# Graph network layer on one core: attention scores in single PSUM banks, and single-row source fetches by SyncE for eleven blocks instead of six

## Chip, core and metric

One core of one Trainium2 chip. The metric is the time of one execution in device microseconds: 1613.16 us in the median of three runs before the change (1609.63 to 1617.16).

## What is computed

```python
ea  = edge_attr @ w_e + b_e                       # 131072 edges, 64 -> 256 features
msg = relu(x[src] + ea)                           # x: 8192 nodes x 256
agg = segment_sum(msg, dst, 8192)                 # dst is sorted
t   = x + agg
h_local = bn1(relu(t @ w1 + b1) @ w2 + b2 + x)
# attention in 256 groups of 32 nodes, 4 heads of 64
q, k, v = split(x @ in_w.T + in_b)
attn = softmax(q @ k.T / 8);  h_attn = bn2((attn @ v) @ out_w.T + out_b + x)
out = h_local + h_attn
out = bn3(out + relu(out @ m_w1 + m_b1) @ m_w2 + m_b2)
return layernorm(x + out)
```

## The kernel before

All is float32. The edges come in 128 **blocks** of 1024 (`BE`), in order of `dst`; a block's sums fall on about 64 nodes. The nodes come in 16 **chunks** of 512, so a chunk goes with 8 blocks. The stages of a block `b`:

- POOL fetches the source rows with 8 gathers of 128 rows (`gather`, line 217) into the tile `xs`, from `x` at first, and from block 20 on from `xb`, a copy of `x` with the edge bias added. Each gather is held back by a semaphore until TensorE has reached a mark in its own list, by planned times (`hold_fetches`).
- SyncE loads the edge features `ea` with four DMAs (`load_edges`, line 264; four buffers).
- VectorE transposes `ea` in 32x32 squares into `eaT` (`edge_transpose`, line 281; two buffers).
- TensorE multiplies `eaT` with the weights (`edge_products`) into two PSUM tiles `pe` of two banks each; the tag `pe` has two buffers, four banks. All matmuls are recorded at line 174.
- VectorE adds `xs` and `pe` (`edge_messages`, line 338, two adds of 1024 columns; called **adds** below), ScalarE applies relu (line 342).
- VectorE builds a one-hot `oh` of the destinations (`edge_hot`, line 350; two buffers), and TensorE sums the messages with it into `pw` (**sums**). ScalarE copies `pw` to `ws` (line 385), and TensorE places `ws` into `l2` with a second one-hot. VectorE adds that to the chunk's `xT` (line 409).

Beside this run, chunk by chunk, the attention (`attention_front`, `attention_back`) and the dense layers with the layer norm (`dense`; its last step is a reciprocal of `rstd`, line 730, and four scalings of `y`, line 732, and SyncE's store of `y`). Their PSUM tiles, `pw` and `l2` have the tag `at`: four buffers of one bank. In `attention_back` the scores of two heads are multiplied into one tile of two banks (`bank2()`, so with the tag `pe`), and ScalarE copies the blocks on its diagonal to `pr` with four copies of 256 columns for two heads (line 617).

**Single rows.** For the blocks in `FETCHED`, the last of the eight gathers is left out, and SyncE fetches these 128 rows with one DMA each from `xb` into a tile `xf` of its own (`row_stream`, line 242; two buffers), 16 rows in a step. A step begins with the load of 16 addresses into registers (line 235). `fetch_rows` allows `RUN` steps per block from block `FROM` on, and `some_rows` issues them. The add of such a block's last quarter is made in three pieces (line 332).

**What sets the order.** TensorE's list is in the order of the code. Up to block 104 (`TAIL`) the code goes by pairs of blocks: sums of block b-2, products of b, sums of b-1, then adds of b, a share of attention and dense work (`Work.run`), one-hot and products of b+1, and so on. From block 104 on, a small planner in the code picks the next piece of work, block by block, by planned times (`came`, `added`, `summed_at`). VectorE's and ScalarE's lists are in the order of the code up to block 24 (`NV`). From there on, and for SyncE throughout, the build's scheduler decides where an instruction stands, by its own planned times and by what an instruction depends on; on the chip each engine then takes its list strictly in order.

Of the kernel before, what the change touches and what calls it, by code (L numbers as in the profile page):

```python
# [19 lines left out]
P = 128  # L20
# [21 lines left out]
RUN = 0.75  # L42
RL = 4
FETCHED = [44, 54, 64, 76, 86, 98]
FROM = 26
# [39 lines left out]
def gnn_kernel(ctx: ExitStack, tc: tile.TileContext, x, src, dst, edge_attr, w, out):  # L85
# [121 lines left out]

    def gather(b):
        xs = epool.tile([P, NH, TJ, C], FP, name="xs", tag="xs", bufs=BUFS)
        for h in range(NH):  # L210
            for j in range(TJ):
                if b in FETCHED and h * TJ + j == TB - 1:
                    continue
                idx = srcd[:, b * NH + h, j : j + 1] if b < ND else srci[:, b, h * TJ + j : h * TJ + j + 1]
                fetches.append((
                    b * TB + h * TJ + j,
                    nc.gpsimd.indirect_dma_start(  # L217
                        out=xs[:, h, j, :],
                        out_offset=None,
                        in_=x if b < NX else xb[:, :],  # L220
                        in_offset=bass.IndirectOffsetOnAxis(ap=idx, axis=0),
                    ).ins,
                ))
# [4 lines left out]
    xf_of = {}  # L228

    def row_stream():  # L230

        for b in FETCHED:
            xf = xf_of[b] = epool.tile([P, C], FP, name="xf", tag="xf", bufs=2)
            for r in range(0, QR, RL):
# [5 lines left out]
                for i, at in enumerate(rows):  # L240
                    p = i % EQ * QR + r + i // EQ
                    nc.sync.dma_start(xf[p : p + 1, :].bitcast(U8), xb_bytes[:, ds(at, C * 4)])  # L242
                yield
# [71 lines left out]
    def edge_messages(b, pairs=range(0, NH, 2), of_pair=range(2)):  # L315
# [6 lines left out]
        for h in pairs:  # L322
            pe = pe_of[b, h]
            for u in of_pair[::n]:
                hs = slice(h + u, h + u + n)
                if h + u + n == NH and b in FETCHED:
                    for us, js, rows in (
# [255 lines left out]
    def attention_back(st, pool, bank, bank2):  # L583
# [18 lines left out]
        for hh in range(H // 2):  # L602
            two = bank2()
            for t in range(TN):
                for s in range(2):
                    a = t * P
                    matmul(
                        two[:, s, a : a + P],
# [5 lines left out]
            two4 = two.rearrange("p s (t k) -> p s t k", t=TN)  # L614
            for g in range(GT):
                q = slice(g * NPG, (g + 1) * NPG)
                nc.scalar.copy(pr[q, :, 2 * hh : 2 * hh + 2, :].rearrange("p t s k -> p s t k"), two4[q, :, :, q])
# [224 lines left out]
    class Work:  # L842
# [69 lines left out]
    with tc.manual_schedule(engines={PE}):  # L912
# [9 lines left out]
        for c in range(NCH):  # L922
# [10 lines left out]
            work.add(BACK, lambda s=st: s.get("front"), attention_back(st, npool, bank, bank2))  # L933
# [116 lines left out]
        came = [8.7 + 10.035 * (i + 1) for i in range(NB)]  # L1050
# [88 lines left out]
    with tc.If(wide > 0):  # L1139
# [67 lines left out]
        with tc.tile_pool(name="gfin", bufs=1) as pool, tc.tile_pool(name="gfin_ps", bufs=1, space=PSUM) as ps_pool:  # L1207
# [4 lines left out]
            def gbank2():  # L1212
                return ps_pool.tile([P, 2, CH], FP, name="gat2", tag="gat2", bufs=2)

            with tc.For_i(0, N, CH) as n0:
# [3 lines left out]
                for _ in attention_back(st, pool, gbank, gbank2):  # L1219
                    pass  # L1220
# [38 lines left out]
```

## Time and profile before

| | |
|---|---|
| median of three runs | 1613.16 us |
| profiled execution, its own time | 1610.6 us |
| its span, first to last instruction | 1608.8 us |
| mean granted TensorE clock | 0.911 |
| bytes read from and written to HBM | 222.13 MB and 16.78 MB |
| share of 16 DMA engines taken by POOL's gathers | 30.9% |
| and by SyncE's queue | 22.6% |

PE is TensorE, PEld its weight loads, DVE VectorE, ACT ScalarE, POOL GpSimd, SP SyncE. A line of a group reads: line, engine, operation, tile written <- tiles read, shapes, count | busy us, mean ns of one | idle us of the engine just before them, with what ended most of it. A line of the timeline reads: start us, length us, engine, line, operation, tiles, shapes, count, and in brackets the idle time before it with what ended it. "Issue" and "remote" are waits whose end the profile can't put down to an instruction. A matmul counts as two records, and its end is modelled. SP and the queues (SPq) have no busy time; their lines show from the first to the last issue. Fetches and transposes are told apart by block by counting them in the lists.

### The profile page before, as it was taken

The numbers are of one execution on the slowest core, as the hardware profiler recorded it, in microseconds if no ns is written. First come the engines' busy times: TensorE is split into PE (matmuls) and PEld (weight loads), VectorE is DVE, ScalarE is ACT, GpSimd is POOL, SyncE is SP. The second block draws the span as 40 slices with busy tenths as digits, with TensorE's granted clock in tenths as the row PEclk, the third lists the DMA queues.
The fourth block names the chain that finished last, engine by engine and source line by source line (L and its number), as shares of the span: only waits on it lengthen the run. The fifth ranks groups of instructions, "written<-read, shape, count | busy, mean of one in ns | idle before, by whom it ended". The sixth has DMA issues, their size and how long they took to land.

```text
span 1608.8 us, 23797 instructions
## 1 busy us (share of the span) xinstructions
PE 1325.8 (82%) x7671; PEld 769.9 (48%) x7671; DVE 804.0 (50%) x1643; ACT 588.3 (37%) x840; POOL 969.5 (60%) x1026
## 2 busy tenths in 40 slices
PE   4887898888988988987778777887788888888887
PEld 2444455444545444544445444454354444445465
DVE  4366554545445453463634536346363463645363
ACT  1333333343425333352433424325243253443233
POOL 6666565665666666666556565655665655666661
PEclk9798899899998999899899898899899999999999
DMA  9698765364645445355463564635548564545431
GB/s 230 181 298 267 215 181 135 112 168 116 170 130 163 126 129 156 99 144 146 122 159 103 150 150 123 160 100 154 144 116 196 141 161 123 158 136 145 118 105 51
DMA packets 150333, 240.57 MB, mean 150 GB/s; under 512 B 28638, under 2 KB 113788, under 8 KB 149436
## 3 DMA queue, kind: packets, MB, share of 16 engines
q0 software_dynamic: 48864, 133.50, 30.9%
q1 hardware_dynamic: 92860, 98.17, 22.6%
q10 hardware_dynamic: 8480, 7.35, 1.6%
q8 instruction: 62, 1.02, 0.3%
q14 instruction: 67, 0.55, 0.1%
HBM read 222.13 MB, written 16.78 MB: 148 GB/s over the span
## 4 chain that ended last, share of the span: by engine, by line
PE 35%; DVE 5%; issue 5%; another core or an unknown queue 3%; DMA 3%; ACT 1%; SPq 1%; POOL 0%; DVEq 0%; ACTq 0%; POOLq 0%
PE at L174 16%; PE pe L174 10%; PE pw L174 4%; PE l L174 3%; DMA xs<-xb,srci 2%; DVE xs L338 1%; PE at L763 1%; PE at L714 1%; DMA ea<-in_edge_attr_dram 1%; DVE eaT L281 1%; SPq L242 1%; DVE y L720 0%; PE at L178 0%; ACT xs L342 0%
## 5 line engine op out<-in xcount | busy, mean ns | idle before, releaser
L217 POOL DMA_INDIRECT xs<-xb,srci x858 | 814.7, 950 | 520.5 <-issue 200.6
L342 ACT ACTIVATE xs<-xs 128x1024 f32<-128x1024 f32 (+2 forms) x253 | 264.2, 1046 | 558.7 <-DVE xs L338 368.7
L338 DVE TENSOR_TENSOR xs<-pe,xs 128x1024 f32<-128x1024 f32 (+2 forms) x253 | 299.4, 1204 | 242.7 <-PE pe L174 72.3
L174 PE MATMUL pe<-we,eaT 64*128 64x256 f32 x2048 | 313.4, 440 | 120.4 <-issue 38.8
L174 PEld LDWEIGHTS pe<-we,eaT 64*128 64x128 f32 x2048 | 221.9, 214 | 231.4 <-issue 152.7
L174 PE MATMUL pw<-xs,oh 128*32 128x256 f32 x2048 | 183.6, 420 | 50.6 <-issue 35.8
L217 POOL DMA_INDIRECT xs<-in_x_dram,srci x144 | 137.5, 955 | 82.1 <-issue 44.0
L350 DVE TENSOR_TENSOR oh<-iota_n,rel 128x128 f32<-128x128 f32 x256 | 64.7, 291 | 212.7 <-PE pw L174 97.3
L174 PEld LDWEIGHTS pw<-xs,oh 128*32 128x32 f32 x2048 | 68.7, 116 | 165.3 <-issue 112.4
L174 PE MATMUL at<-xT,inT 128*128 128x512 f32 x256 | 124.5, 613 | 4.9 <-ACT qk L579 2.8
L174 PE MATMUL at<-hA,mw 128*128 128x512 f32 (+1 forms) x256 | 120.8, 598 | 1.1 <-issue 0.9
L174 PE MATMUL at<-m,mw 128*128 128x512 f32 (+1 forms) x256 | 118.3, 608 | 3.6 <-issue 2.5
L174 PE MATMUL l<-oh,ws 128*128 128x160 f32 (+4 forms) x512 | 88.1, 311 | 23.7 <-issue 11.9
L281 DVE STREAM_TRANSPOSE eaT<-ea 128x512 f32<-128x512 f32 x128 | 89.9, 702 | 32.5 <-PE pe L174 15.1
L409 DVE TENSOR_TENSOR xT<-l,xT 128x352 f32<-128x352 f32 (+14 forms) x107 | 43.4, 428 | 120.3 <-remote 35.7
L174 PEld LDWEIGHTS l<-oh,ws 128*128 128x128 f32 x512 | 75.0, 197 | 47.5 <-issue 28.0
L385 ACT COPY ws<-pw 128x512 f32<-128x512 f32 (+1 forms) x77 | 39.3, 510 | 118.5 <-remote 37.0
L174 PEld LDWEIGHTS at<-xT,inT 128*128 128x128 f32 x256 | 48.1, 195 | 66.4 <-issue 56.0
L174 PEld LDWEIGHTS at<-m,mw 128*128 128x128 f32 x256 | 50.6, 205 | 56.4 <-issue 50.7
L695 ACT ACTIVATE m<-at,vec 128x512 f32<-128x512 f32 (+1 forms) x64 | 41.9, 657 | 87.8 <-PE at L174 30.8
L174 PEld LDWEIGHTS at<-hA,mw 128*128 128x128 f32 x256 | 48.1, 200 | 52.8 <-issue 49.4
L174 PE MATMUL at<-oT,outT 128*128 128x512 f32 x128 | 64.3, 623 | 7.0 <-ACT oT L652 6.1
(157 smaller groups left out, 1295.7 us busy)
## 6 DMA issues: line engine op xcount, KB each, us to landing
ea<-in_edge_attr_dram SPq DMA_DIRECT2D x512, 128.0 KB
xs<-xb,srci POOLq DMA_INDIRECT x858
xf<-xb SPq DMA_DIRECT2D x768, 1.0 KB
xn<-in_x_dram ACTq DMA_DIRECT2D x14, 512.0 KB
out_dram<-y SPq DMA_DIRECT2D x14, 512.0 KB
xp<-in_x_dram SPq DMA_DIRECT2D x10, 512.0 KB
xb<-xp SPq DMA_DIRECT2D x10, 512.0 KB
xp<-in_x_dram SPq DMA_DIRECT2D x3, 1024.0 KB
```

The costliest lines, as they stand in the source:

```text
L174: mark(ps, nc.tensor.matmul(ps, *args, **kw).ins)
L217: nc.gpsimd.indirect_dma_start(out=xs[:, h, j, :], out_offset=None, in_=x if b < NX else xb[:, :], in_offset=bass.IndirectOffsetOnAxis(ap= ...
L242: nc.sync.dma_start(xf[p : p + 1, :].bitcast(U8), xb_bytes[:, ds(at, C * 4)])
L281: nc.vector.transpose(eaT, ea[:, QR:].rearrange("p (g d) -> p g d", d=ED)[:, :, :QR])
L338: nc.vector.tensor_add(msg[:, hs, js].rearrange("p u i c -> p i u c"), pe[:, js, u : u + n, :], xs[:, hs, js].rearrange("p u i c -> p i u c"),
L342: nc.scalar.activation(msg[:, hs, js], msg[:, hs, js], AF.Relu)
L350: nc.vector.tensor_tensor(oh[:, ts], iota_n[:, None, :WN].to_broadcast([P, TB // 2, WN]), rel[:, b, ts, None].to_broadcast([P, TB // 2, WN ...
L385: newest["ws"] = nc.scalar.copy(ws[:, :n], pw[:, :n]).ins
L409: newest["xT"] = nc.vector.tensor_add(xT, l2[:, :, a - n : z - n], xT).ins
L695: newest["relu"] = nc.scalar.activation(m1[:, o, :], layer(mw1, KC, o, hA), AF.Relu, bias=v_("m_b1", o)).ins
L714: nc.tensor.transpose(ps[:wt, t - t2, k * P : (k + 1) * P], zT[:, k, t * P : t * P + wt], ident)
L763: nc.tensor.matmul(ps[i], wt[:, k, o * P : (o + 1) * P], act[:, k, :], start=(k == 0), stop=(k == nk - 1))
```

## The change

1. The scores of two heads go to two tiles of one bank with the tag `at` instead of one tile of two banks with the tag `pe`. ScalarE copies each tile by itself: eight copies of 128 columns for two heads instead of four of 256, so 256 in all instead of 128. `bank2` is no longer handed to `attention_back`.
2. `FETCHED` has eleven blocks, 36, 44, ... 116, instead of 44, 54, 64, 76, 86 and 98, so POOL's gathers are 1013 instead of 1018. The steps begin at block 22 instead of 26, and each block has one instead of three in four blocks: 88 steps and 1408 rows instead of 48 and 768.
3. For the two of these blocks that lie in the tail (108 and 116), later gathers are dated one gather (1.254 us) earlier each, in `gather` and in the tail's `came`, and the planner lets rows be issued after each piece of work (`between()`).

```diff
-RUN = 0.75
+RUN = 1
...
-FETCHED = [44, 54, 64, 76, 86, 98]
-FROM = 26
+FETCHED = list(range(36, 120, 8))
+FROM = 22
...
+    def skipped(b):
+
+        return sum(TAIL <= i <= b for i in FETCHED)
...
-                    b * TB + h * TJ + j,
+                    b * TB + h * TJ + j - skipped(b - 1),
...
-            two = bank2()
+            two = [bank(), bank()]
...
-                        two[:, s, a : a + P],
+                        two[s][:, a : a + P],
...
-            two4 = two.rearrange("p s (t k) -> p s t k", t=TN)
-            for g in range(GT):
-                q = slice(g * NPG, (g + 1) * NPG)
-                nc.scalar.copy(pr[q, :, 2 * hh : 2 * hh + 2, :].rearrange("p t s k -> p s t k"), two4[q, :, :, q])
+            for s, ps in enumerate(two):
+                for g in range(GT):
+                    q = slice(g * NPG, (g + 1) * NPG)
+                    nc.scalar.copy(pr[q, :, 2 * hh + s, :], ps.rearrange("p (t k) -> p t k", t=TN)[q, :, q])
...
                         self.at[i], self.turn = t + 0.5, (i + 1) % n
+                        between()
                         return t
...
-        came = [8.7 + 10.035 * (i + 1) for i in range(NB)]
+        came = [8.7 + 10.035 * (i + 1) - 1.254 * skipped(i) for i in range(NB)]
```

What the build makes of it: TensorE's list is the same up to block 108, but for the names of the score tiles. VectorE's list changes from block 40 on. In the rows below a buffer's number tells the block; lines are those of each version.

VectorE at blocks 48 and 49, before (`oh_4883` is the one-hot of block 48, `eaT_4818` the transpose of block 50, `oh_4971` and `eaT_4904` those of 49 and 51):

```order
L350 TENSOR_TENSOR oh_4883<-iota_n_74,rel_87 128x128 x2
L338 TENSOR_TENSOR xs_4566<-pe_4791,xs_4566 128x2x2x256
L338 TENSOR_TENSOR xs_4566<-pe_4796,xs_4566 128x2x2x256
L281 STREAM_TRANSPOSE eaT_4818<-ea_4340 128x512
L350 TENSOR_TENSOR oh_4971<-iota_n_74,rel_87 128x128 x2
L660 SCALAR_TENSOR_TENSOR hA_3764<-at_4825,s2_101,hA_3764 128x512
L338 TENSOR_TENSOR xs_4575<-pe_4890,xs_4575 128x2x2x256
L338 TENSOR_TENSOR xs_4575<-pe_4895,xs_4575 128x2x2x256
L281 STREAM_TRANSPOSE eaT_4904<-ea_4446 128x512
```

The same place after the change (`eaT_5133` is the transpose of block 48 itself, `eaT_5252` that of 49):

```order
L357 TENSOR_TENSOR oh_5445<-iota_n_74,rel_87 128x128 x2
L287 STREAM_TRANSPOSE eaT_5133<-ea_4615 128x512
L345 TENSOR_TENSOR xs_5079<-pe_5354,xs_5079 128x2x2x256
L345 TENSOR_TENSOR xs_5079<-pe_5359,xs_5079 128x2x2x256
L357 TENSOR_TENSOR oh_5533<-iota_n_74,rel_87 128x128 x2
L667 SCALAR_TENSOR_TENSOR hA_4218<-at_5388,s2_101,hA_4218 128x512
L287 STREAM_TRANSPOSE eaT_5252<-ea_4703 128x512
L345 TENSOR_TENSOR xs_5088<-pe_5452,xs_5088 128x2x2x256
L345 TENSOR_TENSOR xs_5088<-pe_5457,xs_5088 128x2x2x256
```

A block's transpose has moved from behind the adds of two blocks before to directly ahead of its own adds, behind its own one-hot.

VectorE at block 70, where a chunk's layer norm and softmax lie (`eaT_6964`, and after it `eaT_7793`, is the transpose of block 70). Before:

```order
L350 TENSOR_TENSOR oh_7262<-iota_n_74,rel_87 128x128 x2
L281 STREAM_TRANSPOSE eaT_6964<-ea_6572 128x512
L730 RECIPROCAL rstd_7106<-rstd_7106 128x4
L732 TENSOR_SCALAR y_6846<-y_6846,mv_6848,rstd_7106 128x256 x4
L630 TENSOR_REDUCE sm_7173<-pr_7039 128x16
L338 TENSOR_TENSOR xs_6910<-pe_7220,xs_6910 128x2x2x256
L631 RECIPROCAL sm_7173<-sm_7173 128x16
L633 TENSOR_TENSOR pr_7039<-pr_7039,sm_7173 128x128 x4
L338 TENSOR_TENSOR xs_6910<-pe_7225,xs_6910 128x2x2x256
L637 STREAM_TRANSPOSE bd_99<-pr_7039 32x16x32 x4
```

And after:

```order
L357 TENSOR_TENSOR oh_8150<-iota_n_74,rel_87 128x128 x2
L737 RECIPROCAL rstd_7945<-rstd_7945 128x4
L739 TENSOR_SCALAR y_7673<-y_7673,mv_7675,rstd_7945 128x256 x4
L287 STREAM_TRANSPOSE eaT_7793<-ea_7351 128x512
L637 TENSOR_REDUCE sm_8011<-pr_7868 128x16
L638 RECIPROCAL sm_8011<-sm_8011 128x16
L640 TENSOR_TENSOR pr_7868<-pr_7868,sm_8011 128x128 x4
L644 STREAM_TRANSPOSE bd_99<-pr_7868 32x16x32 x4
L345 TENSOR_TENSOR xs_7737<-pe_8058,xs_7737 128x2x2x256
L345 TENSOR_TENSOR xs_7737<-pe_8063,xs_7737 128x2x2x256
```

The transpose was late here already; now the layer norm's last step stands ahead of it as well, and the block's adds stand behind the softmax.

VectorE in the tail, before (`oh_11128` is the one-hot of block 113, `eaT_11053` the transpose of block 114, the adds those of 112):

```order
L350 TENSOR_TENSOR oh_11128<-iota_n_74,rel_87 128x128 x2
L281 STREAM_TRANSPOSE eaT_11053<-ea_10699 128x512
L409 TENSOR_TENSOR xT_9770<-l2_11063,xT_9770 128x2x104
L409 TENSOR_TENSOR xT_10320<-l2_11063,xT_10320 128x2x40
L338 TENSOR_TENSOR xs_10863<-pe_11043,xs_10863 128x2x2x256
```

And after (`oh_13242` is the one-hot of block 113, `eaT_13014` the transpose of block 112, the adds those of 112):

```order
L357 TENSOR_TENSOR oh_13242<-iota_n_74,rel_87 128x128 x2
L287 STREAM_TRANSPOSE eaT_13014<-ea_12464 128x512
L416 TENSOR_TENSOR xT_11132<-l2_13178,xT_11132 128x2x104
L416 TENSOR_TENSOR xT_12085<-l2_13178,xT_12085 128x2x40
L345 TENSOR_TENSOR xs_12995<-pe_13158,xs_12995 128x2x2x256
```

In place of a transpose two blocks ahead, the list has here that of the block whose adds come next, behind the one-hot of the block after it.

More of the change, by code (lines that the diff above doesn't have):

```diff
@@ L242, in row_stream @@
                     nc.sync.dma_start(xf[p : p + 1, :].bitcast(U8), xb_bytes[:, ds(at, C * 4)])
+                if r + RL == QR:
+                    all_of.add(b)
                 yield
@@ L581, in attention_front, with attention_back @@
             yield 1.7
-    def attention_back(st, pool, bank, bank2):
+    def attention_back(st, pool, bank):
         xT, hA, qk = st["xT"], st["hA"], st["qk"]
@@ L932, in gnn_kernel @@
             )
-            work.add(BACK, lambda s=st: s.get("front"), attention_back(st, npool, bank, bank2))
+            work.add(BACK, lambda s=st: s.get("front"), attention_back(st, npool, bank))
             if c < NCH - 2:
@@ L1218, in gnn_kernel @@
                     pass
-                for _ in attention_back(st, pool, gbank, gbank2):
+                for _ in attention_back(st, pool, gbank):
                     pass
```

5 lines of the change are left out of this document (2 added, 3 removed).

## Prediction, made before the changed kernel ran

> **What bounds the kernel now.** I read the page's first part, then busy time by stretches, then who TensorE waited for in each stretch, then single places in order of time.
>
> ```profile
> span 1608.8 us, 23797 instructions
> PE 1325.8 (82%) x7671; PEld 769.9 (48%) x7671; DVE 804.0 (50%) x1643; ACT 588.3 (37%) x840; POOL 969.5 (60%) x1026
> ...
> L217 POOL DMA_INDIRECT xs<-xb,srci x858 | 814.7, 950 | 520.5 <-issue 200.6
> ```
>
> TensorE is the busiest engine. POOL, whose gathers the rows are meant to relieve, stood idle 520.5 us ahead of the 858 gathers from `xb`: it is held back to TensorE's progress and isn't what is short. The trace decides more when it is cut at the starts of the adds of blocks 24, 56, 96 and 120. First everything, then only what touches the transposed edge rows `eaT`; columns: stretch, its length, busy us and (count) of PE, PEld, DVE (in the first fence ACT and POOL too), granted clock, DMA share, GB/s.
>
> ```profile
> 341.50:716.30 374.80, 323.03 (x1811) 182.29 (x1804) 186.82 (x370) 145.83 (x200) 233.98 (x246) 0.90 0.52 138
> 716.30:1220.50 504.20, 394.97 (x2276) 229.97 (x2276) 239.12 (x466) 184.20 (x250) 302.14 (x318) 0.89 0.53 138
> 1220.50:1503.90 283.40, 247.25 (x1440) 140.55 (x1438) 149.21 (x297) 111.55 (x163) 174.29 (x185) 0.95 0.55 146
> ```
> ```profile
> 341.50:716.30 374.80, 72.62 (x512) 49.60 (x512) 21.64 (x31) 0.90 0.52 138
> 716.30:1220.50 504.20, 111.05 (x636) 80.38 (x636) 28.13 (x40) 0.89 0.53 138
> 1220.50:1503.90 283.40, 52.06 (x392) 37.28 (x390) 18.30 (x26) 0.95 0.55 146
> ```
>
> A block has 16 records of products, so 512 are 32 blocks: 374.8 / 32 = 11.71 us a block. The middle stretch has 40 blocks (40 transposes): 504.2 / 40 = 12.61. The last has 24: 283.4 / 24 = 11.81. The work per block is alike in the first two, yet the middle one is **0.90 us a block slower**. What TensorE's products `pe` waited for, in the first stretch and then in the middle one (us in total, times, longest):
>
> ```profile
> PE pe L174 <- issue: 14.8, 16, 4.0
> ...
> PE pe L174 <- DVE eaT L281: 2.4, 1, 2.4
> ```
> ```profile
> PE pe L174 <- DVE eaT L281: 34.7, 10, 6.4
> PE pe L174 <- issue: 26.3, 10, 6.9
> PE pe L174 <- DVE oh L350: 22.8, 6, 5.6
> PE pe L174 <- DVE rstd L730: 10.2, 2, 5.1
> ```
>
> That is 17.2 us against 94.0: the products have begun to wait for VectorE. In VectorE's list of before, the transpose of a block stands right behind the adds of the block two before it, well ahead of need, up to block 53; from 55 to 98 it stands directly ahead of its own block's adds (I call that late), and from 99 on it is early again, which is where the third stretch recovers. Such a wait in order of time:
>
> ```profile
> 1012.46 1.07 PE L174 MATMUL pw<-xs,oh 128*32 128x256 f32 x16
> ...
> 1014.64 0.49 DVE L350 TENSOR_TENSOR oh<-iota_n,rel 128x128 f32<-128x128 f32 x2 [6.36 <-PE pw L174]
> 1015.05 0.70 DVE L281 STREAM_TRANSPOSE eaT<-ea 128x512 f32<-128x512 f32 x1
> ...
> 1015.81 3.68 PE L174 MATMUL pe<-we,eaT 64*128 64x256 f32 x16 [2.29 <-issue]
> ```
>
> The one-hot `oh` needs the buffer that the sums `pw` of two blocks earlier release (1014.64); the transpose stands behind it, and TensorE's next work, the products, behind the transpose: 1015.81 - 1014.64 = 1.17 us in which TensorE has nothing. In a pair this hits the even block alone, since other work stands between the sums and the odd block's products. The middle stretch has about 20 such even blocks; its 0.90 x 40 = 36 us over 20 are **1.8 us a wait**, more than the 1.17 seen as idle.
>
> **The change, part by part.**
>
> *The order of VectorE.* Nothing in the diff names it, but the build places the transposes anew. After the change the transposes are late from block 40 to block 116, not from 55 to 98. Counted in the built order, even blocks whose transpose stands behind their own one-hot: 20 before (56 to 96 without 86), 33 after (42 to 106). 13 more waits x 1.8 = **+23.4**; at 1.17 each, the idle time alone, 15.2. Queued behind the waiting products on TensorE is all that follows in its list, the sums of the odd block first, so ScalarE's copies and VectorE's adds start later by as much; nothing else is ready for TensorE to take in between.
>
> Blocks 107 to 116 lie in the tail, where blocks go one at a time and TensorE's order puts a block's products right behind the sums of the block before, while the transpose now stands behind a one-hot that waits for just those sums. So each of the 10 blocks waits. Trace of before has no such place in the tail; nearest is the row above. 10 x 1.17 = **+11.7**; at least 0, if the tail's other waits (for `ws` and `xT`) cover it, at most 10 x 1.8 = 18.
>
> At blocks 46, 54, 62, 70, 78, 86, 94 and 102 the new order puts the last step of a chunk's layer norm ahead of the transpose. Before, where it was late already:
>
> ```profile
> 988.75 0.56 DVE L350 TENSOR_TENSOR oh<-iota_n,rel 128x128 f32<-128x128 f32 x2 [2.25 <-remote]
> 989.24 0.70 DVE L281 STREAM_TRANSPOSE eaT<-ea 128x512 f32<-128x512 f32 x1
> 989.86 0.13 DVE L730 RECIPROCAL rstd<-rstd 128x4 f32<-128x4 f32 x1
> 990.03 1.38 DVE L732 TENSOR_SCALAR y<-y,mv,rstd 128x256 f32<-128x256 f32 x4
> 990.08 3.36 PE L174 MATMUL pe<-we,eaT 64*128 64x256 f32 x14 [5.13 <-DVE rstd L730]
> ```
>
> Reciprocal and four scalings, 0.13 + 1.38 = 1.5 us, ran beside the products; now they stand between one-hot and transpose, with TensorE waiting. 8 x 1.5 = **+12**; 0 if TensorE still has matmuls in its queue then (its sums were dispatched at 983.88, and the one-hot that waits for them started at 988.75, so a backlog of some us does occur). The same block's adds now follow the softmax too; that delays its messages, which have the rest of the pair's dense work to hide behind.
>
> *Fewer gathers.* 11 blocks instead of 6 leave out a gather: 5 x (0.95 busy + 0.30 to the next one) = 6.3 us less on POOL. I count 0: POOL's idle 520.5 us hide it. The Trainium skill (Trainium Kernel Development and Optimization, Key Constraints) says that DMAs issued by different engines share the same 16 DMA engines, and that issuing from several saves only the issue time. That speaks against a gain here, and the idle row agrees; by it the most that could be had is those 6.3 us.
>
> *SyncE's rows.* 5 x 128 more one-row DMAs, and eight steps per eight blocks in place of six.
>
> ```profile
> L235 SPq TENSOR_LOAD <-last_src x48: 769/1189/2342, 230.4 to 1197.7; - x48
> ...
> ```
> ```profile
> 1005.47 7.38 SPq L242 DMA_DIRECT2D xf<-xb  x16
> 1012.94 1.76 SPq L264 DMA_DIRECT2D ea<-in_edge_attr_dram  x4
> 1016.05 7.97 SPq L242 DMA_DIRECT2D xf<-xb  x16
> ...
> 1053.09 39.88 SPq L242 DMA_DIRECT2D xf<-xb  x16
> 1093.01 1.76 SPq L264 DMA_DIRECT2D ea<-in_edge_attr_dram  x4
> ```
>
> A step with a block's edge loads behind it takes 1016.05 - 1005.47 = 10.6 us of SyncE, and each block now has one: 8 x 10.6 = 85 of the 101 us that eight late blocks take. Before, SyncE ran ahead and stood some 30 us in the row of 39.88 us. So the added rows fill idle time: 0. If steps grow past 12.6 us, SyncE becomes the bound (a rival below). VectorE's add of a block with single rows goes in three pieces instead of one:
>
> ```profile
> L332 DVE TENSOR_TENSOR xs<-pe,xs 128x512 f32<-128x512 f32 (+1 forms) x12 | 6.1, 536 | 2.1 <-PE at L174 2.1
> ...
> L332 DVE TENSOR_TENSOR xs<-pe,xf 128x256 f32<-128x256 f32 x6 | 2.5, 415 | 0.0
> ```
> ```profile
> L338 DVE TENSOR_TENSOR xs<-pe,xs 128x1024 f32<-128x1024 f32 (+2 forms) x253 | 299.4, 1204 | 242.7 <-PE pe L174 72.3 <-remote 46.7 <-PE pw L174 36.9
> ```
>
> 2 x 0.54 + 0.42 - 1.20 = 0.3 us, 5 times: +1.5 if nothing hid it; VectorE idles enough, 0.
>
> *The tail's plan.* Gathers and plan are dated up to two gather times earlier there, and TensorE's order differs from about block 109 on without losing or gaining a matmul. Nearest are the rates 11.71 and 11.81 of the first and third stretch, written by two different planners: 20 blocks x 0.1 = 2 us either way; 0.
>
> *Scores in single banks.* TensorE's records on `qk` with the idle time ahead of them, and ScalarE's copies of the scores:
>
> ```profile
> L174 PE MATMUL pe<-qk x512: 266/272/579, 75.4 to 1433.6; 64*128 64x128 f32 x171
> its engine sat idle before it (us, times) until:
>   issue: 10.2, 8
>   DVE xs L338: 2.1, 3
> ```
> ```profile
> L617 ACT COPY pr<-pe 32x256 f32<-32x256 f32 x128 | 46.3, 362 | 50.2 <-PE at L714 15.9 <-remote 11.4 <-PE pe L174 10.3
> ...
> L566 ACT COPY xT<-at 128x512 f32<-128x512 f32 x32 | 17.9, 580 | 18.6 <-issue 9.2 <-remote 3.7 <-PE at L174 2.3
> ```
>
> No longer waiting for the two `pe` buffers gains 12.3 us at most. Against it stand 256 copies of half the width for 128. Between 362 ns for 256 columns and 580 for 512, 0.85 ns a column, a copy of 128 would be 254 ns (estimate): 256 x 0.254 - 46.3 = 18.7 us more on ScalarE, 37% busy, and the next user of an `at` bank waits for them. Both ends, -12.3 and +18.7, are open; they nearly cancel, I take 0.
>
> **The sum.** 23.4 + 11.7 + 12 = 47.1. The profiled execution took 1610.6 us (span 1608.8), 2.6 below the median of 1613.16: 1610.6 + 47.1 = **1658**, which I also give for the median. Lower ends together: 15.2 - 12.3 - 2 = 1, so 1612; upper: 23.4 + 18 + 12 + 1.5 + 2 + 18.7 = 76, so 1686.
>
> One page would price the waits lower. TensorE: Matmul & The Clock Gate (Part 1, of the Trainium skill) has the array fall to half clock only after an idle window of about 3.4 us; waits of 1.2 us would then cost no clock, and the 13 waits 15.2 instead of 23.4, in all 1650. The clock rows above, 0.89 in the late stretch against 0.90 and 0.95, neither confirm nor exclude that.
>
> **Rivals.**
>
> *The backlog covers it (faster).* A wait costs only from the point where TensorE's queue is empty when the one-hot is released. If that is rarely so, and the middle stretch is slow for another reason such as the granted clock, the order costs nothing and what is left is 12.3 from the scores and 6.3 from POOL: 1592. For it: the 3.8 us of backlog above. Against it: stretch three recovers exactly where the transposes are early again. Chance 0.07.
>
> *Late, but cheap.* The lower ends hold, tail and layer norm are covered, scores gain: 1612. Chance 0.06.
>
> *SyncE becomes the bound.* Decides from 12.6 us a step. At 13.2, blocks 40 to 110 would take 70 x 0.6 = 42 us more: 1700. For it: edge loads wait in SyncE's list behind 16 rows each; against it: 10.6. Chance 0.10.
>
> *Banks.* If ScalarE's copies are waited for at every chunk, their 18.7 us come on top: 1677. Chance 0.12.
>
> The forecast itself: 0.65.
>
> **Range and chances.** 1628 to 1702: it leaves out the two cheap cases (0.13) and about 0.07 beyond 1702. Around what a measurement of this kernel tells from no change, 0.5% or 8 us: faster 0.07, same 0.06, slower 0.87.
>
> **What would show it.** In the changed profile: eight-block periods of about 101 to 103 us from block 42 on, not from 56; products waiting for `eaT`, `oh` and, at the eight layer-norm places, for `y`, from about 550 us to 1480; POOL's idle time larger, not smaller; no waits of `pe<-qk`, and ScalarE's copies near 254 ns. I am wrong if the periods between blocks 42 and 55 stay near 94, or if SyncE shows no stall at all and `eaT` waits for the DMA of `ea`.

## The result and the profile after

The changed kernel took 1764.86 us in the median of six executions (1742.93 to 1781.15), the kernel before 1614.03 beside it. Two of the six fell in a slower state, at 1775 and 1781 us, and are left out here. The other four took 1755 us on average, 142 us more than before: a ratio of **1.088** (95% interval 1.081 to 1.095), so 8.8% slower. The forecast was 1658, with a range up to 1702; 142 us were lost where 47 were worked out. The profiled execution took 1769.03 us, the longest of the four, so its span is 158 us longer than that of before.

From the page of the changed kernel, its span, TensorE's line and three groups (busy us, mean ns of one | idle us ahead of them):

```profile
span 1767.3 us, 25309 instructions
...
PE 1336.8 (76%) x7671; PEld 772.1 (44%) x7671; DVE 813.4 (46%) x1653; ACT 606.7 (34%) x968; POOL 968.0 (55%) x1021
...
L221 POOL DMA_INDIRECT xs<-xb,srci x853 | 813.0, 953 | 666.9 <-issue 183.2
L174 PE MATMUL pe<-we,eaT 64*128 64x256 f32 x2048 | 335.4, 465 | 273.5 <-DVE eaT L287 202.3
...
L624 ACT COPY pr<-at 32x128 f32<-32x128 f32 x256 | 65.7, 257 | 39.7 <-remote 14.4
```

No engine has much more work: TensorE was busy for 1336.8 us, before for 1325.8. All engines wait more. POOL's idle time grew from 520.5 to 666.9, so five gathers fewer gain nothing. The idle time ahead of TensorE's edge products grew from 120.4 to 273.5. The same group before:

```profile
L174 PE MATMUL pe<-we,eaT 64*128 64x256 f32 x2048 | 313.4, 440 | 120.4 <-issue 38.8
```

Busy time by stretches, cut at the starts of the adds of blocks 0, 24, 56, 96 and 120, first the one stretch of before that the prediction did not need, then the changed kernel (columns as in the prediction):

```profile
22.20:341.50 319.30, 267.25 (x1570) 151.38 (x1571) 165.31 (x350) 111.74 (x158) 196.97 (x208) 0.91 0.71 203
```
```profile
21.60:360.30 338.70, 270.07 (x1551) 152.42 (x1553) 165.15 (x351) 116.24 (x190) 197.75 (x208) 0.89 0.68 191
360.30:759.00 398.70, 310.90 (x1824) 174.94 (x1822) 190.34 (x372) 150.22 (x232) 234.45 (x246) 0.91 0.48 128
759.00:1326.90 567.90, 407.35 (x2282) 232.81 (x2280) 243.01 (x470) 190.47 (x290) 301.07 (x316) 0.85 0.45 123
1326.90:1658.30 331.40, 253.30 (x1432) 145.62 (x1430) 150.84 (x302) 113.85 (x185) 173.71 (x183) 0.89 0.49 128
```

The stretches grew by 19.4, 23.9, 63.7 and 48.0 us. Two of these numbers speak against the prediction at once. The first 24 blocks lost 19.4 us though no transpose moved there and no block uses single rows yet. SyncE does begin to fetch rows within this stretch, at 244 us (before at 232), but the kernel with the rows alone, shown below, loses nothing up to here; what costs is the scores in single banks, which was counted at 0. And blocks 56 to 96, where the transposes were late already, lost 63.7, of which the forecast had 9.3. What TensorE waited for in that third stretch, and one line of VectorE's waits (us in total, times, longest):

```profile
PE pe L174 <- DVE eaT L287: 103.2, 22, 13.0
PE pe L174 <- DVE oh L357: 12.5, 2, 6.9
PE at L721 <- ACT pr L624: 8.6, 5, 3.7
```
```profile
DVE oh L357 <- remote: 103.6, 15, 10.5
```

Before, 34.7 us of such waits ended with `eaT`; now 103.2, and one takes up to 13 us where the prediction had 1.2 to 1.8 (the row of before that the prediction shows has 10 of these waits, 3.5 us each on average). "remote" means that the releaser isn't in the trace, but by the code the one-hot waits only for the buffer that the sums `pw` free. The row with the longest wait, in order of time:

```profile
1281.07 1.07 PE L174 MATMUL pw<-xs,oh 128*32 128x256 f32 x16
...
1291.62 0.29 DVE L357 TENSOR_TENSOR oh<-iota_n,rel 128x128 f32<-128x128 f32 x1 [8.65 <-remote]
...
1293.11 1.38 DVE L739 TENSOR_SCALAR y<-y,mv,rstd 128x256 f32<-128x256 f32 x4
1294.40 0.70 DVE L287 STREAM_TRANSPOSE eaT<-ea 128x512 f32<-128x512 f32 x1
...
1295.16 3.31 PE L174 MATMUL pe<-we,eaT 64*128 64x256 f32 x14 [13.02 <-DVE eaT L287]
```

This is the chain that was forecast: sums, one-hot, the layer norm's `y`, transpose, products. What is longer is its first link: the one-hot starts 9.5 us after the modelled end of the sums (1282.14), where the two places that the prediction shows have 1.1 and 3.8 us. The ends of matmuls are modelled, so part of the 13 us may be matmuls that ran later than their records say.

### The profile page after: what moved, and what is told of

Read it like the earlier page. It is cut to its first block, busy times and chain, and to the rows that moved or that the text cites. A ratio compares the mean times of both kernels' runs of the same rounds, so it can differ in the third digit from the quotient of the medians.

```text
span 1767.3 us, 25309 instructions
## 1 busy us (share of the span) xinstructions
PE 1336.8 (76%) x7671; PEld 772.1 (44%) x7671; DVE 813.4 (46%) x1653; ACT 606.7 (34%) x968; POOL 968.0 (55%) x1021
## 3 DMA queue, kind: packets, MB, share of 16 engines
q8 instruction: 62, 1.02, 0.2%
## 5 line engine op out<-in xcount | busy, mean ns | idle before, releaser
L221 POOL DMA_INDIRECT xs<-xb,srci x853 | 813.0, 953 | 666.9 <-issue 183.2
L174 PE MATMUL pe<-we,eaT 64*128 64x256 f32 x2048 | 335.4, 465 | 273.5 <-DVE eaT L287 202.3
L349 ACT ACTIVATE xs<-xs 128x1024 f32<-128x1024 f32 (+1 forms) x248 | 258.7, 1046 | 592.7 <-DVE xs L345 375.8
L345 DVE TENSOR_TENSOR xs<-pe,xs 128x1024 f32<-128x1024 f32 (+1 forms) x248 | 295.0, 1207 | 252.8 <-PE pe L174 78.8
L174 PEld LDWEIGHTS pe<-we,eaT 64*128 64x128 f32 x2048 | 237.9, 228 | 386.7 <-DVE eaT L287 170.9
L174 PE MATMUL at<-m,mw 128*128 128x512 f32 (+1 forms) x256 | 114.7, 592 | 12.1 <-ACT m L702 8.9
L174 PE MATMUL at<-hA,mw 128*128 128x512 f32 (+1 forms) x256 | 116.5, 579 | 4.2 <-DVE hA L696 2.6
L174 PE MATMUL at<-xT,w 128*128 128x512 f32 (+1 forms) x128 | 72.4, 701 | 22.4 <-issue 15.6
L174 PEld LDWEIGHTS l<-oh,ws 128*128 128x128 f32 x512 | 72.8, 193 | 37.2 <-issue 21.8
L624 ACT COPY pr<-at 32x128 f32<-32x128 f32 x256 | 65.7, 257 | 39.7 <-remote 14.4
```

Of the source, the lines that this page charges most:

```text
L174: mark(ps, nc.tensor.matmul(ps, *args, **kw).ins)
L221: nc.gpsimd.indirect_dma_start(out=xs[:, h, j, :], out_offset=None, in_=x if b < NX else xb[:, :], in_offset=bass.IndirectOffsetOnAxis(ap= ...
L345: nc.vector.tensor_add(msg[:, hs, js].rearrange("p u i c -> p i u c"), pe[:, js, u : u + n, :], xs[:, hs, js].rearrange("p u i c -> p i u c"),
L349: nc.scalar.activation(msg[:, hs, js], msg[:, hs, js], AF.Relu)
L624: nc.scalar.copy(pr[q, :, 2 * hh + s, :], ps.rearrange("p (t k) -> p t k", t=TN)[q, :, q])
```

## The experiments

Theory **order**: the late transposes cost the time. Rivals: **banks** (TensorE waits for banks that ScalarE's copies of the scores hold) and **rows** (the single-row DMAs and SyncE's queue cost it themselves). The kernels ran in five sets, each on one chip with the kernel before beside them (the last two sets on the same chip; which chip made the first comparison isn't known), and the chips differ: the kernel before took 1313.0 and 1311.3 us in two sets, but 1597.5, 1614.4 and 1611.8 in the other three, close to the 1614 of the first comparison. I call them quick and slow chips, say for each number which it was, and compare ratios to the kernel before, or times of one set.

### Each part alone

The scores of the change put into the kernel before, on a quick and on a slow chip:

```diff
-            two = bank2()
+            two = [bank(), bank()]
...
-                nc.scalar.copy(pr[q, :, 2 * hh : 2 * hh + 2, :].rearrange("p t s k -> p s t k"), two4[q, :, :, q])
+                    nc.scalar.copy(pr[q, :, 2 * hh + s, :], ps.rearrange("p (t k) -> p t k", t=TN)[q, :, q])
```

> The kernel before with the scores in single banks and nothing else of the change; VectorE's transposes stand where they stood before. Theory 'order' (the late place of the transposes makes the change slow): the late stretch stays near 101 us per eight blocks; at most the 19 us that the changed kernel lost before block 24, so 1614 to 1635. Rival 'banks' (matmuls that wait for ScalarE's narrower copies make it slow): 60 us or more, 1675 and up.

> The kernel before with the scores in single banks alone, once more. On a chip where the kernel before takes 1313 us it cost 11 us. Where that takes 1600, the first 24 blocks of the changed kernels took 329 to 339 us against 319 before, with no row fetched yet: 'banks cost on every chip' expects 1.008 to 1.015 there; 'they are free and the rest of the loss is the rows' expects 1.000 plus or minus 0.005.

Measured: 1.0083 (1.0066 to 1.0100), 11 us, on the quick chip; **1.0397 (1.0369 to 1.0425), 62.5 us**, on the slow one. VectorE's order is that of before in both, but for one transpose and one add that stand a few places elsewhere. So the banks cost. On the slow chip the time, 1676.94, is the one that the first expectation gave for the rival "banks" (1675 and up), against at most 1635 for "order"; the second expectation, 1.008 to 1.015, was far too low.

The other half is the changed kernel with the scores, and their copies, taken back:

```diff
-            two = [bank(), bank()]
+            two = bank2()
```

> The changed kernel with the scores put back into the two-bank tile; all else of the change, and VectorE's late order, is there. Order: eight-block periods near 110 us from block 40 to 116, 1735 to 1765 in all, perhaps 19 less than the changed kernel. Banks: 1690 or less.

> The changed kernel with the scores put back into the two-bank tile, once more. Where the kernel before takes 1313 us it cost 1.041. Where it takes 1600: if banks and rows with their order add up, 1.088 less 0.040, that is 1.045 to 1.055; if each makes the other dearer, less: 1.02 to 1.035.

Measured: 1.0412 (1.0387 to 1.0437) on the quick chip, where 1735 to 1765 could not come up since the kernel before took 1313; **1.0453 (1.0418 to 1.0488), 74 us**, on the slow one. There that is 1685.88, which is not what "order" expected either, but within "banks" (1690 or less). On the slow chip the parts add up: 0.0397 + 0.0453 = 0.085, beside the 0.088 (0.081 to 0.095) of the change. The changed kernel itself on a quick chip:

> The changed kernel itself, beside the kernel before on whatever chip these runs get: in the first set of runs the kernel before took 1313 us where it had taken 1613, so the cost has to be read anew as a ratio. Theory 'order and banks add up' (scores alone 1.008, rows with the late order 1.041): 1.04 to 1.06 on a chip where the kernel before takes 1313. Theory 'the cost is a share of the time, whatever the chip': 1.088 again.

Measured: 1.0565 (1.0543 to 1.0587), 72 us, so the first theory; a little more than the parts' 0.0495. By stretches, the rows alone and then the scores alone on the slow chip, from the starts of blocks 40, 56 and 96 (the last ends at block 120):

```profile
523.60:729.20 205.60, 151.65 (x892) 91.25 (x892) 97.42 (x190) 73.09 (x100) 120.68 (x128) 0.90 0.49 134
729.20:1254.90 525.70, 393.10 (x2282) 229.75 (x2282) 243.88 (x470) 184.12 (x250) 297.69 (x315) 0.87 0.49 131
1254.90:1577.80 322.90, 252.88 (x1432) 146.78 (x1429) 150.51 (x301) 110.12 (x161) 173.06 (x183) 0.89 0.50 133
```
```profile
543.40:742.30 198.90, 160.77 (x894) 88.39 (x892) 92.75 (x188) 75.02 (x116) 121.39 (x128) 0.91 0.48 128
742.30:1282.50 540.20, 403.92 (x2282) 234.01 (x2282) 239.41 (x466) 190.09 (x290) 301.47 (x317) 0.86 0.50 129
1282.50:1570.40 287.90, 248.18 (x1438) 139.93 (x1437) 148.97 (x297) 114.52 (x187) 173.15 (x184) 0.94 0.53 141
```

Before, these stretches took 191.6, 504.2 and 283.4. Rows: +14.0, +21.5, +39.5. Banks: +7.3, +36.0, +4.5, and block 40 starts 18.7 us later (543.4 against 524.7). With the rows alone it starts at 523.6, so what is lost ahead of block 40 is the banks', though in both kernels rows are being fetched by then. The banks cost most where the transposes are late: 36 us for the 40 blocks of the middle.

### Copies or banks

Before, with the two-bank tile kept and only the copies made narrow:

```diff
-            for g in range(GT):
+            for s in range(2):
+                for g in range(GT):
...
+                    nc.scalar.copy(pr[q, :, 2 * hh + s, :], two[:, s].rearrange("p (t k) -> p t k", t=TN)[q, :, q])
```

> The kernel before with its scores still in the two-bank tile, but copied out by 256 copies of 128 columns in place of 128 of 256, as the changed kernel does. The scores in single banks cost 1.040 where the kernel before takes 1614 us, and 1.008 where it takes 1313. If the longer time of ScalarE's copies is what costs: the same again. If it is that TensorE's next work must wait for a shared bank that the copies hold: 0.998 to 1.008 on either.

Measured on the slow chip: 1.0016 (0.9992 to 1.0039). The copies by themselves are free; the **shared banks** cost. TensorE's and POOL's lists are the same in this kernel and in the one with single banks, and VectorE's and ScalarE's differ in a few places only. Who waited for the copies (us, times), in this kernel and then in the one with single banks, both on slow chips:

```profile
who waited for it (us, times):
  DVE mx L623: 25.6, 4
  PEld pe L174: 8.1, 2
  PE pe L174: 7.4, 2
```
```profile
who waited for it (us, times):
  DVE mx L623: 22.7, 3
  PEld at L714: 17.9, 8
  PE at L714: 15.8, 8
  PEld l L174: 8.5, 4
  PE l L174: 7.7, 4
```

A copy takes as long in both, 257 and 256 ns. In the two-bank tile only the next products stand behind it. In the ring of four `at` banks, the sums, the placements `l` and every layer of the dense work do, and TensorE's list is in the order of the code. With two smaller rows of that view, TensorE's matmuls waited 29.9 us for the copies. One step later it waited longer for `eaT`, 58.8 us in the whole run against 37.0 before, so part of the loss shows there; the two together are 52 of the 62.5 us. On the quick chip the same waits for copies come to 37.2 us, and the kernel lost only 11: what a wait costs depends on what else fills the time.

### The price of a late transpose

No single rows at all, and the same with transposes put late by hand in blocks 40 to 102:

```diff
-FETCHED = [44, 54, 64, 76, 86, 98]
+FETCHED = []
```
```diff
     def edge_products(b, pairs=range(0, NH, 2)):
+        if 40 <= b <= 103:
+            if b not in hot_ins:
+                edge_hot(b)
+            with tc.issue_after(hot_ins[b]):
+                next_edges(b, True)
```

> The kernel before with no single rows at all, all gathers by POOL; every transpose is early. Order: before's own late stretch (blocks 55 to 98) goes, ratio 0.97 to 0.985. Against the run with late transposes and no rows, 1.010 where the kernel before took 1313 us, it gives what 63 late blocks cost alone. If POOL's gathers are what the rows have to relieve: above 1.01.

> The kernel before with no single rows at all (all gathers by POOL) and the transposes of blocks 40 to 102 put behind their own one-hots, as the changed kernel has them. Order: 63 blocks at 13.9 us where early ones take 11.7, so about 110 us per eight blocks there and 1690 to 1730 in all. Rows: no single row is fetched, so periods below 98 and 1600 or less.

> No single rows, transposes early, no doubled products; the base for the next run. 1.003 where the kernel before takes 1313 us; where it takes 1600 and POOL has idle time, leaving its late stretch out should gain: 0.96 to 0.99.

> The run before with the transposes of blocks 40 to 102 late, without doubled products. It cost 10 us over its base where the kernel before takes 1313 us, and 74 us with doubled products where that takes 1600. 'The chip sets the price' expects 60 to 90 us over its base where the kernel before takes 1600, and 10 again where it takes 1313; 'only the doubled work sets it' expects 10 to 25 on both.

Measured on quick chips: 1.0034 (1.0015 to 1.0054) and 1.0098 (1.0081 to 1.0115), in different sets. On one slow chip: **0.9797 (0.9772 to 0.9822)** and 1.0010 (0.9993 to 1.0027), that is 1581.35 and 1615.23, 33.9 us apart. Of what was expected, 0.96 to 0.99 came true; 1690 to 1730, 0.97 to 0.985 on the quick chip, and both ranges for the late transposes on the slow one, 60 to 90 and 10 to 25 us, were missed. Blocks 40 to 104, early and late, first the slow chip, then quick ones (columns as before):

```profile
521.60:1283.90 762.30, 643.08 (x3640) 365.73 (x3639) 374.98 (x740) 291.53 (x400) 486.53 (x512) 0.94 0.54 144
```
```profile
522.30:1316.20 793.90, 626.71 (x3662) 369.12 (x3659) 387.17 (x740) 294.06 (x400) 482.66 (x510) 0.89 0.52 139
```
```profile
418.90:1064.40 645.50, 588.73 (x3662) 349.31 (x3659) 377.88 (x739) 291.86 (x400) 488.77 (x515) 0.94 0.65 171
```
```profile
422.40:1078.20 655.80, 579.17 (x3662) 343.75 (x3661) 383.01 (x740) 292.23 (x400) 494.81 (x520) 0.97 0.65 171
```

31.6 us over 63 late blocks is **0.50 us a block** on the slow chip; 10.3 us is 0.16 on the quick ones. POOL is busy for 488.77 of 645.50 us there, and with 0.30 us to the next gather, 1.25 us each, 512 gathers take 640: POOL sets the pace, and TensorE has time to spare for the waits. With early transposes its products waited 42.9 us for the adds in this stretch; with late ones they waited 59.6 for `eaT` and only 7.2 for the adds. To see a late transpose without that spare time, each edge product was done twice:

```diff
-                for i, rows in enumerate(half):
+                for i, rows in list(enumerate(half)) * (2 if b >= NX else 1):
```

> No single rows, transposes early, and each edge product from block 20 on is done twice (the second writes the same values again), so that TensorE gets about 2 us more work a block. POOL's gathers take 10.03 us a block, and early blocks ran at that pace (80.3 us per eight): if they set the pace there, TensorE now does, at 11 to 11.5 us a block, and the whole takes 1420 to 1470. It is the base for the next run.

> The run before with the transposes of blocks 40 to 102 late. Theory 'slack': where POOL sets the pace TensorE has about 1 us a block to spare, which covers the late waits (they cost 10 us for 63 blocks without the doubling); with TensorE as the bound they cost their full 0.6 to 1.2 us a block, 38 to 75 us over the run before. Rival 'fixed price': 10 us over it again, with or without the doubling.

Measured, both on one slow chip: 0.9926 (0.9907 to 0.9945) and 1.0386 (1.0323 to 1.0448), that is 1586.44 and 1660.35: 73.9 us, **1.17 us a late block**, against 0.50 without the doubled work. That is the size that "slack" expected. On slow chips the spare time isn't POOL's pace, since POOL stood idle for 477 us ahead of its gathers without the doubled products; it is TensorE's own. In blocks 40 to 104 of the early kernels it was idle for 762.3 - 643.1 = 119 us without the doubled work and for 768.5 - 716.9 = 52 with it. The two pairs ran on two slow chips. That the doubled products cost little there was not expected (last section).

### Transposes early in the changed kernel

First by force: one-hots and adds issued behind the newest transpose.

```diff
+        if NV <= b < SPLIT:
+            behind.enter_context(tc.issue_after(turned_ins[max(turned_ins)]))
```

> The changed kernel, all rows and single banks included, with one addition: each block's one-hot and adds are issued on VectorE after the newest transpose traced so far, so that the transpose of a block stands ahead of the adds of the block before it, throughout. Order: eight-block periods back to 92 to 98 us, 1590 to 1640. Rival 'rows' (the single-row DMAs and SyncE's queue themselves make it slow; the transposes would then wait for the DMA of ea): 1720 or more.

Measured: 1.0949 (1.0931 to 1.0967), slower than the change's own 1.0565, though the products no longer wait for `eaT`. It is no test of order, since it moved more than the transposes. From its page, and below it the same group of the rows alone:

```profile
L174 PE MATMUL pw<-xs,oh 128*32 128x256 f32 x2048 | 160.1, 414 | 141.8 <-issue 94.2
...
L423 DVE TENSOR_TENSOR xT<-l,xT 128x352 f32<-128x352 f32 (+14 forms) x107 | 43.9, 434 | 175.3 <-PE l L174 175.1
```
```profile
L416 DVE TENSOR_TENSOR xT<-l,xT 128x352 f32<-128x352 f32 (+14 forms) x107 | 43.8, 432 | 81.0 <-PE l L174 80.8
```

The build now put half of the placements into `xT` one block earlier, ahead of the adds of a pair's second block. VectorE waited there, 175.3 against 81.0 us, and TensorE stood idle for 141.8 us ahead of the sums that need these adds, where the rows alone had 0.3.

Then by cause. The build puts the transposes late because the edge loads stand behind rows in SyncE's list; taken to ScalarE's queue, they let it place the transposes early by itself (all, the middle's, or the tail's):

```diff
-                nc.sync.dma_start(
+                (nc.scalar if b >= 30 else nc.sync).dma_start(
```

with `30 <= b < 104` and `b >= 104` for the other two.

> The changed kernel with the edge loads from block 30 on issued by ScalarE's queue instead of SyncE's, behind no rows; the build then places every transpose early, as in a kernel without rows, while all rows and the single banks stay. Order: the late stretch recovers, ratio 1.00 to 1.02. Rival 'rows' (the single-row DMAs themselves, or adds that wait for them): 1.04 or more. ScalarE issues 4 more DMAs a block, about 2 us of it; if that is what is short, its copies and relus show it.

> The changed kernel with the edge loads of blocks 30 to 103 issued by ScalarE's queue: transposes early up to block 105, late in the tail. Order: what blocks 40 to 103 lose, some 25 to 35 us (684 us from block 40 to 104 in the changed kernel, 649 with all edge loads on ScalarE's queue), is back: 1350 to 1360. If the middle costs nothing on this chip: within 10 us of 1384.

> The changed kernel with the edge loads from block 104 on issued by ScalarE's queue; the build then places the transposes of the tail early again, those of blocks 40 to 103 stay late; rows, plan and single banks stay. If the late order in the tail is what it loses there: 25 to 36 us below the changed kernel (1345 to 1360 where that takes 1384). If the rows or the dates of the plan are: within 10 us of 1384.

Measured: all early 1.0223 (1.0205 to 1.0242), just outside the 1.00 to 1.02 expected, on the quick chip that gave the change 1.0565; middle early **1.0355 (1.0293 to 1.0416)** and tail early 1.0794 (1.0731 to 1.0857), on a slow one. The change itself was not run in that set; the first comparison, on a slow chip too, has 1.088 for it. By that the middle's order is worth about 0.052, some 83 us, with rows and banks left in, far more than the 25 to 35 that the quick chip let expect; the tail's 0.008, less than these intervals tell apart. The middle-early kernel from blocks 40, 56 and 96:

```profile
541.40:736.30 194.90, 156.77 (x911) 87.64 (x908) 94.55 (x189) 74.58 (x116) 119.94 (x127) 0.91 0.50 141
736.30:1237.70 501.40, 407.92 (x2296) 224.85 (x2288) 237.08 (x472) 189.18 (x292) 300.62 (x317) 0.90 0.49 136
```

501.4 against 567.9 in the change and 504.2 before. That is more than the 0.50 us a block of a late transpose alone (20 us for 40 blocks). The same blocks, 56 to 96, with the same rows and early transposes, but two-bank scores (the version at the end of this section):

```profile
719.40:1211.10 491.70, 410.16 (x2294) 232.04 (x2286) 235.85 (x471) 183.76 (x252) 301.80 (x317) 0.91 0.51 139
```

So single banks cost 501.4 - 491.7 = 10 us here where the transposes are early, and 567.9 - 525.7 = 42 where they are late (the change against the rows alone): late transposes make the banks' waits dear. These runs come from different slow sets, whose kernels before differ by 1%, 5 us in such a stretch.

Some of the quick chip's remaining 0.022 may be the new queue. In the kernel with all edge loads on ScalarE, between 987 us and the end, ScalarE stood 36 us in seven waits that ended with a load of `ea`, among them:

```profile
ACT pr L624 <- DMA ea<-in_edge_attr_dram: 11.9, 2, 7.2
...
ACT ws L392 <- DMA ea<-in_edge_attr_dram: 9.3, 2, 5.5
...
ACT oT L659 <- DMA ea<-in_edge_attr_dram: 5.8, 1, 5.8
```

### The tail

```diff
-FETCHED = list(range(36, 120, 8))
+FETCHED = list(range(36, 104, 8))
```

> The changed kernel with the list ended at block 100: nine blocks of single rows instead of eleven, no rows in the tail, transposes late from 40 to 101 and early from there on as before. If the tail (rows of 108 and 116 with late transposes, blocks 104 to 120) is where the rows lose, as in the run of the rows alone (96 to 120 took 269 us, against 232 with the scores alone): 25 to 35 us below the changed kernel. If the loss lies in blocks 40 to 96: within 10 us of it.

Measured: 1.0272 (1.0244 to 1.0300), 36 us below the change in the same set: on the quick chip half of the loss is in the tail. What TensorE waited for most from block 96 on, in the change on that chip and then here:

```profile
PE pe L174 <- DVE eaT L287: 34.2, 19, 5.4
```
```profile
PE pe L174 <- DVE eaT L287: 2.8, 2, 1.4
```

Whether late transposes, the rows of 108 and 116 or the plan's dates cost this is not told apart fully: with early transposes and all rows (all edge loads on ScalarE) the quick chip took 265 us from block 104 on, the change 277, the list up to 100 only 248.

### A version without the three losses

Two-bank scores, nine blocks up to 100, edge loads on ScalarE's queue:

> A version made from what the runs showed: scores in the two-bank tile, nine blocks of single rows (36 to 100, none in the tail), edge loads from block 30 on by ScalarE's queue, so that every transpose is early. If order, banks and tail are all that the change lost: no slower than the kernel before, 0.98 to 1.00. If the rows themselves or ScalarE's DMA issues cost something: 1.01 or more.

Measured: 0.9948 (0.9929 to 0.9968) on a slow chip, 8 us or 0.5% faster than before. No rows at all (0.9797 in the same set) is better there by 25 us, but 1.0034 on a quick chip. So on this slow chip rows don't pay, at least not with the edge loads moved to ScalarE for them; the two were not taken apart.

## Why the prediction was wrong

1. **"Scores in single banks ... nearly cancel, I take 0": this step failed**, and its bounds too. It measured +62.5 us, with +18.7 as upper end. The bound was made from what the copies take on ScalarE, which costs nothing (1.0016). It had to be made from who stands behind a bank: before, only the products, which waited 0.9 us for copies, afterwards all of TensorE's list. The rival "Banks", 0.12 at 1677, named the mechanism and used the same wrong price. It is 62.5 of the 95 us that were missed (142 less 47); the rows with their order, 74 where 47 were worked out, are another 27.
2. **The tail, +11.7, and the sum of the rows, 47.1, were too small.** By stretches from blocks 40, 56 and 96 the forecast had 15.6 (seven waits, two layer norms), 9.3 and 22.2; the rows alone measured 14.0, 21.5 and 39.5, and 28.4 of the last lie between blocks 104 and 120. The first, where the late order is new, came out near; whether by the price of 1.8 us a wait isn't shown (next point).
3. **The price of a wait, 1.8 us, was not a constant.** Late transposes alone cost 0.16, 0.50 or 1.17 us a block by what else fills the time, so twice that for a pair, in which the prediction saw one wait. Its lower price, 1.17, was read from the start of the one-hot on; the row that it comes from shows TensorE idle for 2.29 us. The prediction put the whole 0.90 us by which before's middle was slower down to its even blocks; without rows early blocks take 762.3 / 64 = 11.9 us and late ones 12.4, so late transposes explain about 0.5 of it, and what the rows add to it was not seen. Layer norm in front of the transpose (+12) is in the chain above, but was not priced by itself.
4. **Added, not multiplied.** Terms were summed as if independent. Rows and banks add up (0.085 of 0.088), but within each, order decides the price: the middle's order alone is 34 us without rows and banks, and about 83 with them, and in blocks 56 to 96 the banks cost 10 us with early transposes and 42 with late ones.
5. **What held.** The order itself: late from block 40, early again from 117 on. POOL's gathers: no gain, idle time 666.9. SyncE not the bound: VectorE stood idle ahead of the transposes for the DMA of `ea` for 4.4 us in all. ScalarE's copies: 257 ns, estimated 254. The waits of the score matmuls: 1.8 us are left of 12.3. The periods came from block 42 on as forecast, but longer: 108 us per eight blocks from 40 to 56 and 114 from 56 to 96, not 101 to 103. Late transposes do cost little on quick chips, but there POOL's pace covers the waits, not the backlog on TensorE that the rival "The backlog covers it" named.
6. **The clock.** By the Trainium skill (TensorE: Matmul & The Clock Gate, Part 1) waits under some 3.4 us would cost no clock. The quick chip agrees: in the change's blocks 56 to 96 products waited 30 times for `eaT`, 1.7 us on average and only once above 3.4 (3.6), and the granted clock from block 40 to 104 was 0.98. On the slow chip waits reached 13.0 and the clock was 0.85 where before had 0.89; without rows, late transposes with waits of up to 8.7 us had 0.89 where early ones had 0.94. Which is cause and which effect stays open.

Open too: why the same change costs 72 us on one chip and 142 on another. The granted clock alone doesn't say it: it was 0.971 and 0.885 for the change on the two, 10% apart, while the spans, 1380.7 and 1767.3 us, are 28% apart.

## What to carry to other kernels

Price a bank that moves into a shared ring by what stands behind it in the in-order engine's list, not by the time of the copy that frees it; a change of copies alone tells the two apart in one run. When a build places an in-order engine's instructions, look for what it believes to be late (here the edge loads behind rows in one queue) and move that, rather than force the order: the force cost 1.095, the moved loads 1.022. A price read from one stretch holds only for what bounds that stretch; measure it with the slack taken away as well.

## What the runs showed of the hardware

**The chips differ by 23%, and the difference sits around TensorE.** POOL's gathers, VectorE's transposes and ScalarE's copies take the same time on both (953 and 952 ns, 702 and 703, 257 and 255, in the change on either), while the records of the same 7671 matmuls come to 1336.8 us on the slow chip and 1198.1 on the quick one. And on the slow chip what waits for TensorE starts late. The changed kernel on the quick chip, same kind of place as the chain above:

```profile
794.74 1.07 PE L174 MATMUL pw<-xs,oh 128*32 128x256 f32 x16
...
795.96 0.49 DVE L357 TENSOR_TENSOR oh<-iota_n,rel 128x128 f32<-128x128 f32 x2 [0.41 <-PE pw L174]
796.37 0.70 DVE L287 STREAM_TRANSPOSE eaT<-ea 128x512 f32<-128x512 f32 x1
797.12 2.00 PE L174 MATMUL pe<-we,eaT 64*128 64x256 f32 x16 [1.31 <-DVE eaT L287]
```

Here the one-hot starts 0.15 us after the sums' modelled end, there 9.5. Over all of ScalarE's copies `ws` that were waited for, the median from the modelled end of the sums to the start of the copy was 0.20 us in this run and 0.63 in the change on the slow chip, 2.0 in the kernel before there. This fits a TensorE that runs behind its records on those chips, so that a chain that goes through it and back pays for that each time; since the ends are modelled, the traces don't show it directly.

**Doubled products cost little on slow chips.** The busy times without and with them, both without rows and early:

```profile
PE 1322.8 (84%) x7671; PEld 765.2 (49%) x7671; DVE 796.9 (51%) x1631; ACT 586.2 (37%) x840; POOL 978.7 (62%) x1032
```
```profile
PE 1443.7 (91%) x9399; PEld 894.5 (56%) x9399; DVE 805.3 (51%) x1631; ACT 585.7 (37%) x840; POOL 977.3 (62%) x1032
```

121 us more of busy TensorE, and a ratio of 0.9926 against 0.9797, some 20 us. The granted clock rose from 0.935 to 0.969. POOL wasn't the bound (idle 486 us ahead of its gathers), nor were VectorE and ScalarE. The two runs were made on two chips, but the kernel before had nearly the same median clock there, 0.915 and 0.917, so the chip alone hardly explains it. That a busier TensorE is granted more clock isn't a rule by these runs, though: on the quick chips, in blocks 40 to 104 above, the early kernel kept TensorE busy for 91% of the time at 0.94, the late one for 88% at 0.97. Why the clock rose here stays open.
